# Attention with a top-1 expert branch on one core: the split of the row maxima put ahead of the pair's transfer, and the layernorm's inverse root moved to GpSimd

## The chip, the core and the metric

One core of a Trainium2 chip runs the whole kernel. The metric is device time in microseconds (us) for one execution, inputs and outputs in the chip's memory; lower is better. Engines are named as the profile names them: PE is TensorE's matmuls and PEld its weight loads, DVE is VectorE, ACT is ScalarE, POOL is GpSimd, SP is SyncE, which here only issues transfers.

## The reference

The input x has shape (4, 2048, 512), float32. It is layer-normalised without scale or offset; the attention of 16 heads of width 32 and a top-1 mixture of 8 experts with room for 100 tokens each both read the normalised tokens, and the output is the sum of x and both.

```python
def _layernorm(x, axis=-1, eps=1e-05):
    m = jnp.mean(x, axis=axis, keepdims=True)
    v = jnp.var(x, axis=axis, keepdims=True)
    return (x - m) / jnp.sqrt(v + eps)
...
        scores = jnp.einsum('bhqd,bhkd->bhqk', q, k) / math.sqrt(dh)
        attn = jax.nn.softmax(scores, axis=-1)
        out = jnp.einsum('bhqk,bhkd->bhqd', attn, v)
...
    x = L0_attn_x
    xn = _layernorm(x, axis=-1)
    x = x + _L0_attn_ref(xn, ...) + _L0_ffn_ref(xn, ...)
```

Queries and keys also pass a spectral filter, which the kernel folds into their weights at the start. The softmax subtracts each row's maximum before it exponentiates.

## The kernel before, in words

**Tiling.** The attention is done for one batch and four heads at a time: 4 x 4 = 16 such groups, `k` from 0 to 15. A group has four blocks of 512 queries (`n`), so there are 64 blocks. A block runs over 16 key tiles of 128 keys, two by two: an `even` and an `odd` tile make a window, 8 windows to a block, 512 in all. Scores stand with keys on the partitions and queries along the row.

**One window** (the loop at line 908). For each of its two tiles and each half of the four heads, PE first writes the negated row maxima into the PSUM bank (`shift`, line 614: a matmul with ones against `negms`, a bfloat16 tile), then adds the scores (`scores`, line 603). ACT exponentiates the bank into the tile (line 930). PE multiplies the tile before with the values (`products`, line 630), and DVE adds the result into `num`. For the softmax's sums, the pair of tiles is added: `pair` (line 892) is a transfer issued on POOL that adds the 1 MB `odd` tile onto the `even` one, and `add_to` (line 895) adds the even tile of the window before onto it, mostly on POOL. `odd` tiles have three buffers, `even` tiles five.

**The maxima** are computed ahead. A list `stream` (line 449) has one item for every 128 queries by 512 keys by two heads; the first 40 items run before the window loop (line 788), and after that each half of a tile does one item (`max_matmuls` on PE, `max_reduce` on DVE), so that the maxima of a block are complete some windows before it starts. When a block's 32 items are done, `max_negate` reduces them on DVE, and a window later `max_close` (line 489) turns them on PE and lets ACT copy them twice, as bfloat16 into `row[:, 0]` and as float32 into `rest`. In the window after that, `max_split` (line 501) takes them apart into three bfloat16 parts: two subtractions and two casts on POOL, with three small transfers of 4 KB on SP that spread the three rows into `negms`, the first for ACT's copy, the second and third behind POOL's casts.

**What sets the order.** The engines behind `on` are wrapped by `InOrder` (line 71): each keeps the order in which the program was written, and nothing is rescheduled. So the order in the window loop is the order of POOL's queue: at the head of a window first `pair` (line 910), then `max_split` if a block's maxima are due (line 912), then `add_to` (line 914). What else is to be done is in `agenda`, a list of steps for each window which `plan` (line 841) fills: projections of the next group, loads of weights, the closing of a block (`close_steps`, line 649), the tokens of the next batch. Half of a window's steps follow its even tile, half its odd tile.

**The token stage** (line 221) normalises a batch: `load` (1 MB of x on SP), `measure` (mean and variance on DVE into `mv`), `scale` (line 244: the inverse root of the variance into `rstd`, and `shift`, minus the mean times it), `normalize` on ACT and `turn`, which transposes on PE into `xnT`. For batch 0 this is the start of the kernel, with `scale` for four tiles of tokens at a time and `shift` on DVE (lines 739 to 756). For the other batches it lies in the agenda over the last two groups of the batch before; `scale` then runs once for 16 tiles, with `shift` on POOL. The expert branch gathers at most 800 tokens (7 tiles) and has a `scale` of its own (line 551). ACT's `Sqrt` and `Exp` are in different tables, so that a table load stands before the first Sqrt at the start, and before and after each Sqrt between exponentials. At item 30 of the first loop a one-element `Exp` (line 792) brings in the table of the exponentials early.

Of the kernel before, what the change touches and what calls it, by code (L numbers as in the profile page):

```python
# [12 lines left out]
F32 = mybir.dt.float32  # L13
BF16 = mybir.dt.bfloat16
I32 = mybir.dt.int32
AF = mybir.ActivationFunctionType
ALU = mybir.AluOpType
# [8 lines left out]
P = 128  # L26
NT = S // P
# [7 lines left out]
ST = -(-SLOTS // P)  # L35
NTAB = 4
FAR = 1 << 20
EPS = 1e-5
# [63 lines left out]
def attention_and_top1_experts(ctx: ExitStack, tc: tile.TileContext, a: dict, out: bass.AP):  # L102
    nc = tc.nc
# [4 lines left out]
    const = ctx.enter_context(tc.tile_pool(name="const", bufs=1))  # L108
# [8 lines left out]
    def bank():  # L117

        return array[:, next(turns), :]
# [18 lines left out]
    ones = const.tile([P, P], F32, name="ones")  # L138
    nc.gpsimd.memset(ones, 1.0)
    ones_b = const.tile([P, P], BF16, name="ones_b")  # L140
    nc.gpsimd.memset(ones_b, 1.0)
    eps = const.tile([P, 1], F32, name="eps")
    nc.gpsimd.memset(eps, EPS)

    carry = const.tile([P, E], F32, name="carry")
    nc.gpsimd.memset(carry, 0.0)
# [9 lines left out]
    def chunk(name):  # L156
        tag, bufs = ("y", 1) if name == "y" else ("xs", None)
        return chunks.tile([P, TQ, DM], F32, tag=tag, name=name, bufs=bufs)
# [25 lines left out]
    on = SimpleNamespace(sync=nc.sync)  # L184
# [36 lines left out]
    def token_stage(b):  # L221
        stats = small.tile([P, NT, 6], F32, name="stats")
        mv = small.tile([P, NT, 2], F32, name="mv")
        rstd = small.tile([P, NT], F32, name="rstd")
# [18 lines left out]

        def scale(first=0, last=NT, shift_on=None):
            at = slice(first, last)
            on.scalar.activation(rstd[:, at], mv[:, at, 1], AF.Sqrt, bias=eps[:, 0:1])
            on.vector.reciprocal(rstd[:, at], rstd[:, at])
            if shift_on:
                shift_on.scalar_tensor_tensor(
                    out=shift[:, at], in0=mv[:, at, 0], scalar=-1.0, in1=rstd[:, at], op0=ALU.mult, op1=ALU.mult  # L250
                )
                return
            on.gpsimd.tensor_tensor(shift[:, at], mv[:, at, 0], rstd[:, at], ALU.mult)
            on.gpsimd.tensor_scalar(shift[:, at], shift[:, at], -1.0, None, ALU.mult)
# [205 lines left out]
    def max_matmuls(item, half):  # L460
        k, n, m, t, u = item
        for h in range(2):
            at = DH * (2 * u + h)
            on.tensor.matmul(
                array[:, half[h], :],
                lhsT=qs[k, n][at : at + DH, t * P : (t + 1) * P],
                rhs=ks[k][at : at + DH, m * QB : (m + 1) * QB],
                start=True,
                stop=True,
            )  # L470
# [13 lines left out]
    def max_negate(k, n):  # L484
        negs[k, n] = small.tile([P, HG * TQ], F32, name="neg")
        part = parts.pop((k, n)).rearrange("p h t m -> p (h t) m")
        on.vector.tensor_reduce(negs[k, n], part, AX.X, ALU.max, negate=True)
# [13 lines left out]
    def max_split(k, n):  # L501

        rest, row = closed.pop((k, n))
        for i in (1, 2):
            on.gpsimd.tensor_tensor(rest, rest, row[:, i - 1, :], ALU.subtract)
            on.gpsimd.tensor_copy(row[:, i, :], rest)
        negms[k, n] = qkv.tile([P, QB], BF16, tag="negm", name="negm", bufs=3)
        for i in range(3):
            on.sync.dma_start(out=negms[k, n][i::DH, :], in_=row[:, i, :])


    taken = {}

    def expert_steps():


        def begin():
            w_exp = chunk("w_exp")
            on.sync.dma_start(out=w_exp, in_=a["L0_ffn_w_expert"].rearrange("(r p) n -> p r n", p=P))
            b_exp = work.tile([P, DM], F32, tag="b_exp", name="b_exp", bufs=1)  # L520
            on.sync.dma_start(out=b_exp, in_=a["L0_ffn_b_expert"].partition_broadcast(P))
            entries = small.tile([P, NTAB, ST, 2], F32, name="entries")
            for i, table in enumerate(tables):
                on.sync.dma_start(out=entries[:, i], in_=table.rearrange("(t p) c -> p t c", p=P))
            entry = small.tile([P, ST, 2], F32, name="entry1")
            for i, op in enumerate((ALU.min, ALU.max)):
                on.vector.tensor_reduce(
                    entry[:, :, i], entries[:, :, :, i].rearrange("p n t -> p t n"), AX.X, op
                )
            who = small.tile([P, ST], I32, name="who")  # L530
            on.vector.tensor_copy(who, entry[:, :, 0])
            xg = [chunk("xg"), small.tile([P, ST - TQ, DM], F32, name="xg1")]
            for half in xg:
                on.gpsimd.memset(half, 0.0)
            mv = small.tile([P, ST, 2], F32, name="mv1")
            index = [bass.IndirectOffsetOnAxis(ap=who[:, i : i + 1], axis=0) for i in range(ST)]
            bound = {"bounds_check": B * S - 1, "oob_is_err": False}
            taken.update(mv=mv, w_exp=w_exp, b_exp=b_exp, entry=entry, index=index, bound=bound, xg=xg)

        def row(i):  # L540
            return taken["xg"][i // TQ][:, i % TQ, :]

        def fetch(i):
            on.gpsimd.indirect_dma_start(row(i), None, rows, taken["index"][i], **taken["bound"])

        def measure(i):
            stats = small.tile([P, 6], F32, name="stats1")
            on.vector.bn_stats(stats, row(i))
            on.vector.bn_aggr(taken["mv"][:, i, :], stats)

        def scale():
            rstd = small.tile([P, ST], F32, name="rstd1")
            on.scalar.activation(rstd, taken["mv"][:, :, 1], AF.Sqrt, bias=eps[:, 0:1])
            on.vector.reciprocal(rstd, rstd)
            shift = small.tile([P, ST], F32, name="shift1")
            on.gpsimd.tensor_tensor(shift, taken["mv"][:, :, 0], rstd, ALU.mult)
            on.gpsimd.tensor_scalar(shift, shift, -1.0, None, ALU.mult)
            taken.update(rstd=rstd, shift=shift)

        def expert(i):  # L560

            if i >= 2:
                at = slice(i - 2, i - 1)
                pe = bank()
                for r in range(NR):
                    on.tensor.matmul(
                        pe,
                        lhsT=taken["xt"][:, r * P : (r + 1) * P],
                        rhs=taken["w_exp"][:, r, :],
                        start=(r == 0),  # L570
                        stop=(r == NR - 1),
                    )
                on.vector.tensor_tensor(row(i - 2), pe, taken["b_exp"], ALU.add)
            if 1 <= i <= ST:
                px = bank()
                for r in range(NR):
                    on.tensor.transpose(px[:, r * P : (r + 1) * P], row(i - 1)[:, r * P : (r + 1) * P], ident)
                taken["xt"] = work.tile([P, QB], F32, tag="byx", name="xt", bufs=1)
                on.scalar.copy(taken["xt"], px)
            if i >= 2:  # L580
                on.scalar.activation(row(i - 2), row(i - 2), AF.Copy, scale=taken["entry"][:, at, 1])
            if i < ST:
                at = slice(i, i + 1)
                on.scalar.activation(
                    row(i), row(i), AF.Identity, bias=taken["shift"][:, at], scale=taken["rstd"][:, at]
                )

        return begin, fetch, measure, scale, expert

    def gather_row(i):  # L590
# [197 lines left out]
    for i, item in enumerate(stream[:MAX_AHEAD]):  # L788
        if i == 30:

            early = small.tile([P, 1], F32, name="early")
            on.scalar.activation(early, eps, AF.Exp)
        half = next(turns), next(turns)
        max_matmuls(item, half)
        max_reduce(item, half)
        if i in ahead:
            ahead[i]()
        while full_blocks:
            closing[i + 2] = full_blocks.pop(0)
            max_negate(*closing[i + 2])  # L800
        if i in closing:
            max_close(*closing[i])
            max_split(*closing[i])
# [88 lines left out]
    def pair(first, second):  # L892
        on.gpsimd.dma_start(out=first, in_=second, accum_op=ALU.add)
# [5 lines left out]
    pairs, adds, full, splits = {}, {}, {}, {}  # L899
    left = None  # L900
    window = 0
    maxima = stream[MAX_AHEAD:]
    for k in range(B * NG):
        plan(k)
        for n in range(NQ):
            num = work.tile([P, QB], F32, tag="num", name="num")
            tiles = {}
            for w in range(NW):
                even, odd = w * WIN, w * WIN + 1
                if window in pairs:  # L910
                    pair(*pairs.pop(window))
                if window in splits:
                    max_split(*splits.pop(window))
                if window in adds:
                    add_to(*adds.pop(window))
                here = agenda[window]
# [83 lines left out]
```

## Time and profile before

| | |
|---|---|
| median of 3 runs | 4525.47 us (4524.64 to 4526.17) |
| the profiled execution's own time | 4519.14 us |
| its span, first to last instruction | 4517.2 us |
| mean granted clock of TensorE | 0.987 |
| DMA packets | 707.03 MB, mean 157 GB/s |
| pair transfers on POOL | 510 of 1 MB, 8.1 us from issue to landing (median) |
| `even` added on POOL, 128x1024 | 876 of 2517 ns, 2118.2 us busy |
| exponentials on ACT, 128x512 | 4096 of 601 ns |
| subtract and cast of the split, 16x128 | 128 of 417 ns and 128 of 287 ns (mean) |
| table loads on ACT | 11 of 1283 ns |
| Sqrt of 128x4, 128x16, 128x7 | 8 of 284 to 309 ns |

A line of the profile's groups names the engine, the operation and the tiles (written <- read), the count, and then the busy time, the mean of one in ns, the idle time of the engine just before, and what ended it. Most instructions are issued through the wrapper and so have its line, L82; they are told apart by their tiles. In a timeline a line has the start in us, the duration, engine, operation and tiles, how many alike follow each other (x8), and in brackets the idle time before the first and what ended it. `POOL DMA_DIRECT2D` is the issue of a transfer on POOL, not the transfer; `SPq` is an issue on SP. q0 is the queue of POOL's transfers, q1 that of SP's. [...]

### The profile page before, as it was taken

Reading aid. Unit: us, or ns where it says so; the run is one execution under the profiler, and the core shown is the slowest. Engines: PE = TensorE matmul, PEld = TensorE weight load, DVE = VectorE, ACT = ScalarE, POOL = GpSimd, SP = SyncE. Lnnn points to the kernel's source line nnn. Section 1 sums busy time; section 2 is a strip of 40 time slices with the busy share of each in tenths; the row PEclk is TensorE's granted clock in tenths of the full one; section 3 lists DMA queues with packets and bytes.
Section 4 is the critical chain, followed back from the end, with each engine's and each line's share of the span. In section 5 each row is a group of like instructions: output and inputs, shape, how many; then the busy total and the mean of one; then the engine's idle time right before and its main releaser. Section 6 shows DMA issues by size and latency. Waiting matters only on the chain. (4 is left out here: it accounts for less than half of the span.)

```text
span 4517.2 us, 106256 instructions
## 1 busy us (share of the span) xinstructions
PE 4390.0 (97%) x44398; PEld 1883.0 (42%) x44398; DVE 3134.8 (69%) x3642; ACT 2596.8 (57%) x4988; POOL 2919.2 (65%) x1993
## 2 busy tenths in 40 slices
PE   8999999999999999999999999999999999999998
PEld 4343433434434343444444434343443434434432
DVE  6667667766676777776666766677667765777776
ACT  3455555575555555557555555556655555555555
POOL 0677666765766666775676656667567665776673
PEclk9999999999999999999999999999999999999999
DMA  4677778886777777897677777789767866787778
GB/s 107 157 165 156 152 144 163 196 196 129 144 153 149 145 156 152 167 215 168 131 147 149 159 140 142 156 177 208 160 130 159 167 141 127 149 169 157 149 157 176
DMA packets 191546, 707.03 MB, mean 157 GB/s; under 512 B 47374, under 2 KB 52656, under 8 KB 125784
## 3 DMA queue, kind: packets, MB, share of 16 engines
q0 software_dynamic: 110432, 605.83, 68.9%
q1 hardware_dynamic: 79456, 93.89, 6.7%
q8 instruction: 347, 5.69, 0.5%
q14 instruction: 135, 1.11, 0.1%
q10 hardware_dynamic: 1176, 0.52, 0.0%
HBM read 76.03 MB, written 89.98 MB: 37 GB/s over the span
## 5 line engine op out<-in xcount | busy, mean ns | idle before, releaser
L82 DVE TENSOR_REDUCE part<-array 128x2 f32<-128x1024 f32 (+1 forms) x2313 | 2434.8, 1097 | 1251.7 <-PE array L82 1239.6
L82 PE MATMUL array<-k,q 32*128 32x512 f32 x8192 | 2242.4, 626 | 4.6 <-issue 2.2
L82 POOL TENSOR_TENSOR even<-even 128x1024 f32<-128x1024 f32 x876 | 2118.2, 2517 | 183.0 <-DMA even<-odd 181.8
L82 PE MATMUL array<-q,k 32*128 32x512 f32 x8192 | 2068.7, 598 | 0.8 <-issue 0.8
L82 ACT ACTIVATE even<-array 128x512 f32<-128x512 f32 x2048 | 1066.3, 601 | 540.9 <-PE array L82 536.7
L82 ACT ACTIVATE odd<-array 128x512 f32<-128x512 f32 x2048 | 1060.1, 602 | 429.0 <-issue 221.4
L82 POOL DMA_DIRECT2D even<-odd x510 | 442.0, 867 | 1227.6 <-ACT odd L82 1032.7
L82 PEld LDWEIGHTS array<-k,q 32*128 32x128 f32 x8192 | 811.3, 185 | 165.6 <-DVE num L82 68.4
L82 PE MATMUL array<-negm,ones_b 3*128 3x512 bf16 x4096 | 799.1, 384 | 78.7 <-DMA negm<-row 70.5
L82 PEld LDWEIGHTS array<-q,k 32*128 32x128 f32 x8192 | 755.3, 187 | 16.5 <-issue 6.8
L82 DVE TENSOR_TENSOR num<-num,array 128x512 f32<-128x512 f32 x960 | 651.2, 678 | 50.5 <-PE array L82 31.2
L82 PEld LDWEIGHTS <-ones_b 3*128 3x128 bf16 x4096 | 203.4, 92 | 968.7 <-issue 805.5
L82 PE MATMUL array<-even,v 128*32 128x512 f32 x4096 | 549.6, 607 | 14.4 <-ACT odd L82 14.4
L82 PE MATMUL array<-odd,v 128*32 128x512 f32 x4096 | 555.3, 613 | 4.7 <-ACT even L82 4.5
L82 PE MATMUL array<-xnT,wg 128*32 128x512 f32 x4096 | 465.5, 595 | 1.3 <-ACT xnT L82 0.7
L82 PE MATMUL array<-wo,ot 128*32 128x512 f32 x2048 | 259.3, 596 | 1.7 <-POOL ot L82 1.7
L82 PEld LDWEIGHTS array<-xnT,wg 128*32 128x32 f32 x4096 | 132.7, 111 | 307.2 <-issue 271.1
L82 PEld LDWEIGHTS array<-odd,v 128*32 128x32 f32 x4096 | 81.9, 109 | 405.6 <-ACT even L82 397.2
L82 PEld LDWEIGHTS array<-even,v 128*32 128x32 f32 x4096 | 81.1, 108 | 406.4 <-ACT odd L82 393.5
L82 PEld LDWEIGHTS array<-wg,xnT 128*32 128x32 f32 x8192 | 226.2, 110 | 41.4 <-issue 23.8
L82 PE MATMUL array<-wg,xnT 128*32 128x128 f32 x8192 | 235.7, 273 | 1.9 <-issue 1.9
L82 ACT COPY y<-array 128x512 f32<-128x512 f32 x252 | 147.7, 586 | 138.3 <-PE array L82 137.7
(127 smaller groups left out, 1354.5 us busy)
## 6 DMA issues: line engine op xcount, KB each, us to landing
even<-odd POOLq DMA_DIRECT2D x510, 1024.0 KB, 8.1
out_dram<-y POOLq DMA_DIRECT2D x63, 1024.0 KB, 12.1
xs<-in_L_attn_x_dram SPq DMA_DIRECT2D x30, 1024.0 KB
out_dram<-xs SPq DMA_DIRECT2D x16, 1024.0 KB
factor<-inverse SPq DMA_DIRECT2D x248, 64.0 KB
wg<-wd SPq DMA_DIRECT2D x15, 768.0 KB
wo<-in_L_attn_w_out_dram SPq DMA_DIRECT2D x16, 256.0 KB
negm<-row SPq DMA_DIRECT2D x192, 4.0 KB
```

Of the source, the lines that this page charges most:

```text
L82: done = act(*args, **kwargs)
```

## The change

At the head of a window the split now comes before the pair. And the inverse root is computed on POOL as (variance + eps) to the power -0.5, with a constant tile of exponents; ACT's Sqrt and DVE's reciprocal are gone, with the table loads around them. The early `Exp` reads another constant, as `eps` is no longer a tile.

```diff
-    eps = const.tile([P, 1], F32, name="eps")
-    nc.gpsimd.memset(eps, EPS)
+    power = const.tile([P, NT], F32, name="power")
+    nc.gpsimd.memset(power, -0.5)
...
         def scale(first=0, last=NT, shift_on=None):
             at = slice(first, last)
-            on.scalar.activation(rstd[:, at], mv[:, at, 1], AF.Sqrt, bias=eps[:, 0:1])
-            on.vector.reciprocal(rstd[:, at], rstd[:, at])
+            on.gpsimd.tensor_scalar(rstd[:, at], mv[:, at, 1], EPS, None, ALU.add)
+            on.gpsimd.tensor_tensor(rstd[:, at], rstd[:, at], power[:, at], ALU.pow)
...
             rstd = small.tile([P, ST], F32, name="rstd1")
-            on.scalar.activation(rstd, taken["mv"][:, :, 1], AF.Sqrt, bias=eps[:, 0:1])
-            on.vector.reciprocal(rstd, rstd)
+            on.gpsimd.tensor_scalar(rstd, taken["mv"][:, :, 1], EPS, None, ALU.add)
+            on.gpsimd.tensor_tensor(rstd, rstd, power[:, 0:ST], ALU.pow)
...
-            on.scalar.activation(early, eps, AF.Exp)
+            on.scalar.activation(early, ones[:, 0:1], AF.Exp)
...
                 even, odd = w * WIN, w * WIN + 1
+                if window in splits:
+                    max_split(*splits.pop(window))
                 if window in pairs:
                     pair(*pairs.pop(window))
-                if window in splits:
-                    max_split(*splits.pop(window))
                 if window in adds:
```

On the engines, the built programs differ in this: POOL's queue has the four instructions of the split ahead of the pair's issue in 63 places (block 0's split lies before the window loop and is unchanged) and 16 more instructions for the eight inverse roots. ACT has eight Sqrt and nine table loads less, DVE eight reciprocals less. The orders on PE and SP are the same.

## The prediction

> **What bounds the kernel now.** I read the page first, then the waits, then the timeline around the longest wait, then the DMA view and the windows view there. The chain that ended last holds only the final few microseconds and says nothing here. The page:
>
> ```profile
> span 4517.2 us, 106256 instructions
> PE 4390.0 (97%) x44398; PEld 1883.0 (42%) x44398; DVE 3134.8 (69%) x3642; ACT 2596.8 (57%) x4988; POOL 2919.2 (65%) x1993
> ```
>
> PE (TensorE's matmuls) is busy for 97%; what can be won is its idle time, and time in which it is busy at a lower clock. The waits:
>
> ```profile
> PE array L82 <- DMA negm<-row: 70.5, 22, 7.0
> PE array L82 <- ACT odd L82: 14.4, 11, 2.2
> POOL even L82 <- ACT odd L82: 1032.7, 307, 12.1
> ```
>
> (waiting instruction <- releaser: us in total, times, longest.) Of some 114 us of PE idleness between matmuls, 70.5 us in 22 waits are for one small transfer: the negated row maxima, which the first `shift` matmul of a block of 512 queries needs. There are 64 such blocks (I count from 0), so about every third stalls. The timeline of block 61 on POOL, then PE:
>
> ```profile
> 4315.71 4.68 POOL L82 TENSOR_TENSOR even<-even 128x1024 f32<-128x1024 f32 x2 [3.59 <-DMA even<-odd]
> 4320.33 0.84 POOL L82 DMA_DIRECT2D even<-odd  x1
> 4320.91 0.42 POOL L82 TENSOR_TENSOR rest<-rest,row 16x128 f32<-16x128 f32 x1
> 4321.40 0.28 POOL L82 CAST row<-rest 16x128 bf16<-16x128 f32 x1
> 4321.76 0.42 POOL L82 TENSOR_TENSOR rest<-rest,row 16x128 f32<-16x128 f32 x1
> 4322.24 0.28 POOL L82 CAST row<-rest 16x128 bf16<-16x128 f32 x1
> ```
>
> ```profile
> 4327.71 0.61 PE L82 MATMUL array<-negm,ones_b 3*128 3x512 bf16 x2 [4.97 <-DMA negm<-row]
> ```
>
> The pair's 1 MB transfer is issued at 4320.33, the four instructions of the split follow and end at 4322.52, SyncE issues the last row at 4322.55, and PE gets it only at 4327.71, 5.2 us later. The DMA view of 4321.6 to 4326.7 and of the microsecond after it (queue: packets, MB, share) says why:
>
> ```profile
> q0 software_dynamic: 128, 1.05, 101.2%
> ```
>
> ```profile
> q1 hardware_dynamic: 40, 0.01, 4.4%
> ```
>
> In the first stretch only the pair's 128 packets move; every packet of the two rows (q1) stands behind them. In block 0, where no pair is under way, the last row is issued at 94.45 and PE starts at 96.70: 2.25 us. So the pair costs a row 3 us, and the split before it on POOL stands behind the pair as well.
>
> The third view is the windows view after the stall of block 20 (3.43 us):
>
> ```profile
> 1490.90:1497.70 6.80, 6.21 (x32) 2.64 (x36) 2.46 (x3) 2.17 (x4) 4.87 (x3) 0.50 0.80 161
> 1497.70:1504.50 6.80, 6.80 (x64) 2.41 (x60) 3.10 (x4) 3.75 (x7) 1.81 (x3) 1.00 0.00 0
> ```
>
> The second column after the stretch is PE with its number of matmuls; 0.50 and 1.00 are the granted clock. After the stall 6.8 us pass at half clock and 32 matmuls run where 64 run next: 3.4 us more are lost. The records show 121 us at half clock in all (mean 0.987); about 88 us of that follow the 22 stalls, a loss of 44 us. [...] I count the half-clock stretches as recorded.
>
> **The split ahead of the pair.** Nothing is added or removed: two subtracts (0.42) and two casts (0.28), 1.60 us with their gaps, change places with one issue (0.6 us until POOL goes on). SyncE's order is the same; its row transfers are only released earlier, with what stands behind them. The split needs ACT's copies of `row` and `rest`, done 3.3 us before the odd exponentials for which the pair waits. But POOL isn't free for all of that: it still adds. New start of the split = the later of ACT's copy and the end of POOL's work before the pair. Block 8: copy at 645.66, POOL's adds end 647.74, so 647.74 to 649.34 instead of 649.58 to 651.18: 1.84 us earlier. Block 16: POOL is busy until 1215.87, so 0.59. For the 22 stalled blocks it is 0.5 to 1.9 us: little.
>
> The larger part is the queue. The last row would be issued 0.03 us after the split, and its first packet comes 1.17 us after its issue (block 0). The pair would be issued as the split ends, and its first packet comes 1.43 us later (median of 148 pairs issued while the engines were quiet). So the row is ahead by about 0.2 us, and it lands 2.25 us after its issue instead of 5.2. [...] I take the row of block 61: first to arrive goes first.
>
> Need against arrival: the stalled blocks want the maxima 9.03 us after ACT's copy in most cases. New arrivals are (split's end) 3.7 to 5.9 + 2.3 = 6.0 to 8.2. So:
> - 16 blocks of the ordinary kind: 44.5 us of stalls go, but for 0.3 (block 24, behind the 768 KB of `wg`).
> - Blocks 60, 61, 63 (4.1 + 5.0 + 7.0 = 16.1 us): POOL is free only 5.2 to 6.7 us after the copy; arrivals are 0.3, 1.5 and 4.5 late. 9.8 us go.
> - Blocks 12, 28, 44 (3.5 + 3.6 + 2.7 = 9.9 us): there the next 1 MB of x stands ahead of the rows on the same queue, and even the first row, issued early, takes 7.5 to 9.8 us to its first packet. These I leave: 0.
>
> Sum 54 us. With these stalls go some 60 us of half-clock stretches (3.4 or 6.8 each): 30 us.
>
> What it costs: the pair starts up to 1.6 us later (block 16: 1217.5 for 1215.9). Next on POOL are adds whose start doesn't move, since split and pair precede them either way. The pair's landing (8.1 us on the page) is wanted one window, about 8.2 us, later, so POOL may wait up to 1.6 us more there. Cover: POOL waits 1032.7 us in all for exponentials, 2 us a pair. Taken as 0; if the cover were gone, see the third rival.
>
> **The inverse root.** Removed: nine of eleven table loads of 1283 ns, eight Sqrt of 0.3 us on ACT, eight reciprocals of 0.2 us on DVE. Added on POOL: eight adds (nearest row: a scalar operation of 128x16 at 0.27 to 0.31 us) and eight powers. No row shows a power. Lower bound: a two-operand POOL instruction of this shape, 0.22 us; below that there is nothing, as an instruction is added. [...] I take 0.5 us.
>
> Mid-kernel the loads stand between two tiles of exponentials:
>
> ```profile
> 923.29 1.28 ACT L82 ACT_TABLE_LOAD   x1
> 924.59 0.31 ACT L82 ACTIVATE rstd<-mv,eps 128x16 f32<-128x16 f32 x1
> 924.92 1.28 ACT L82 ACT_TABLE_LOAD   x1
> ```
>
> PE then waits 1.61 to 1.64 us, four times. Three of these lie just before the waits of blocks 12, 28 and 44, which I leave; there the maxima merely get waited for longer. The fourth counts: 1.6 us. On POOL add and power come before `shift`, which ends at 931.46, while the first normalisation runs at 943.27: 11.8 us of cover. Behind them stand `ot` (wanted by PE 4.6 us after its end) and a pair: hidden up to some 4 us. At the start the chain runs mv 21.92, table load, Sqrt, reciprocal, shift 24.96, normalisation 24.99; ACT would be free at 22.95. With add and power on idle POOL the shift is ready at about 23: 2 us, and 0.7 us on each of three further groups, partly hidden: 3 us. [...]
>
> **Sum.** 54 + 30 + 1.6 + 3 = 89 us against the profiled execution's 4519.1 (span 4517.2 and 1.9 around it). The median of the runs, 4525.5, lies 6.3 us above; the same difference gives 4436.5, I say 4437.
>
> **Rivals.**
> - The x queue clears too (chance 0.10): blocks 12, 28, 44 lose their 9.9 us, 4.9 us of table waits and 8.5 us of half clock: 4413. For it: less traffic in front. Against: the first row's own 7.5 us.
> - The rows still stand behind the pair (0.22): a lead of 0.2 us is small. Then only the earlier split counts, the smaller of lead and stall in 19 blocks: 19 us; shorter stalls save about 10 us of clock; with 4.6 for the root: 4491.
> - The change doesn't do what it says (0.06): the maxima were not late but something just behind them is; the waits are renamed: about 4520.
> - Slower (0.10): the pair's delay takes the place of the wait. Place: POOL's adds, and through the buffers that they free the exponentials and PE. Price: up to 1.6 us in 63 blocks, 101 us, with half clock after some. It decides once POOL's wait for exponentials falls below 1.6 us a window, as it does where POOL is already waiting for a pair (block 61 above: 3.59). All 63 together, against 89 gained and with 30 of clock given back: about 4568.
> The main case holds 0.52.
>
> About 0.2% is what a measurement of this kernel can tell from no change. Faster 0.86, within it 0.05, slower 0.09. The range leaves out the last two rivals: 4408 to 4493.
>
> **What would show it.** Right: the waits of PE for `negm` fall from 70.5 to about 16 us, in blocks 12, 28, 44, 61 and 63; a mean clock of 0.993 or 0.994; last row to matmul 2.3 us; two table loads; powers of about 0.5 us. Wrong: 5 us from the last row to the matmul still (second rival), more of POOL's waiting for `even<-odd` than 191.5 us and PE waiting for exponentials (slower), or powers of many microseconds.

## The result, and the profile after

The changed kernel takes 4455.08 us (median of 4 runs, 4451.27 to 4463.09) against 4525.06 (4 runs, 4524.62 to 4526.17): a ratio of 0.9847, 95% interval 0.983 to 0.9864, some 70 us less. The execution that was profiled took 4463.09 us, the longest of the four, so its span falls by only 55.9 us. Its page:

```profile
span 4461.3 us, 106253 instructions
PE 4369.7 (98%) x44398; PEld 1869.5 (42%) x44398; DVE 3130.6 (70%) x3634; ACT 2581.3 (58%) x4971; POOL 2958.8 (66%) x2009
```

PE is busy 20.3 us less, with the same number of matmuls, and idle between them for 79 us where it was 114. The mean granted clock (TensorE's, which the profile gives as a share of full speed) rises from 0.987 to 0.993. The waits, the same view as before:

```profile
PE array L82 <- DMA negm<-row: 4.6, 3, 3.0
PE array L82 <- POOL ot L82: 37.4, 15, 6.8
PE array L82 <- ACT odd L82: 8.3, 8, 2.2
POOL even L82 <- ACT odd L82: 887.8, 262, 11.9
POOL even L82 <- DMA even<-odd: 241.8, 167, 6.9
```

The wait for the maxima has gone from 70.5 us in 22 stalls to 4.6 in 3. PE's wait for `ot` (the product `num` x `factor`, which closes a block and is made on POOL) was this before:

```profile
PE array L82 <- POOL ot L82: 1.7, 1, 1.7
```

It is now 37.4: about half of the idle time that was won came back under another name. POOL waits less for exponentials (1032.7 before) and more for its pairs (191.5).

Block 61 on POOL, then PE's next stall there:

```profile
4267.53 4.67 POOL L82 TENSOR_TENSOR even<-even 128x1024 f32<-128x1024 f32 x2 [3.57 <-DMA even<-odd]
4272.16 0.42 POOL L82 TENSOR_TENSOR rest<-rest,row 16x128 f32<-16x128 f32 x1
4272.64 0.28 POOL L82 CAST row<-rest 16x128 bf16<-16x128 f32 x1
4273.00 0.42 POOL L82 TENSOR_TENSOR rest<-rest,row 16x128 f32<-16x128 f32 x1
4273.48 0.28 POOL L82 CAST row<-rest 16x128 bf16<-16x128 f32 x1
4273.98 0.88 POOL L82 DMA_DIRECT2D even<-odd  x1 [0.21 <-ACT odd L82]
...
4279.20 1.57 POOL L82 TENSOR_TENSOR ot<-num,factor 128x512 f32<-128x512 f32 x1
```

```profile
4280.82 1.07 PE L82 MATMUL array<-wo,ot 128*32 128x512 f32 x8 [2.10 <-POOL ot L82]
```

The split now ends before the pair's issue. The last row's first packet comes 1.16 us after the row's own issue; before it was 4.30 in this block. Over all 64 blocks the median of that time falls from 4.40 to 1.16 us: before, 62 blocks were above 4 us, now none is, and 52 are at 1.3 or less. In this block the pair is issued 0.21 us after the split ends, and its first packet comes 0.48 us after the row's first one; the row's last packet has come by then (1.27 us after the row's issue). What is left in this block is a wait of 0.88 us for the maxima, which ends at 4275.51, and the stall of 2.10 us for `ot`, behind POOL's adds.

The three longest new stalls are those of blocks 12, 28 and 44. This is block 12, where the inverse root of the next batch runs on POOL as well:

```profile
915.22 4.68 POOL L82 TENSOR_TENSOR even<-even 128x1024 f32<-128x1024 f32 x2 [3.50 <-DMA even<-odd]
920.00 0.27 POOL L82 TENSOR_SCALAR rstd<-mv 128x16 f32<-128x16 f32 x1
920.35 2.94 POOL L82 TENSOR_TENSOR rstd<-rstd,power 128x16 f32<-128x16 f32 x1
...
923.94 1.26 POOL L82 TENSOR_TENSOR ot<-num,factor 128x512 f32<-128x512 f32 x1
```

```profile
925.25 2.79 PE L82 MATMUL array<-wo,ot 128*32 128x512 f32 x12 [6.21 <-POOL ot L82]
```

POOL waits 3.50 us for its pair, adds for 4.68, spends 3.9 on the inverse root and `shift`, and only then divides. PE has been idle for 6.21 us by then; in blocks 28 and 44 it is 6.75 and 5.96 us. The windows view of the 6.8 us from there, with the same columns as before:

```profile
925.20:932.00 6.80, 6.75 (x40) 2.38 (x44) 1.16 (x2) 2.21 (x5) 5.57 (x4) 0.61 1.00 269
```

The granted clock falls to a mean of 0.61 after this stall, as it fell after those for the maxima. The powers, by shape (count, us busy, mean ns):

```profile
L82 POOL TENSOR_TENSOR rstd<-rstd,power 128x16 f32<-128x16 f32 x3 | 8.8, 2943 | 0.2
L82 POOL TENSOR_TENSOR rstd<-rstd,power 128x4 f32<-128x4 f32 x4 | 4.2, 1041 | 0.3
L82 POOL TENSOR_TENSOR rstd<-rstd,power 128x7 f32<-128x7 f32 x1 | 1.5, 1517 | 0.1
```

Two table loads are left of eleven.

### The profile page after: what moved, and what is told of

It reads as the page before. It is cut to its first block, busy times and chain, and to the rows that moved or that the text cites. A ratio compares the mean times of both kernels' runs of the same rounds, so it can differ in the third digit from the quotient of the medians.

```text
span 4461.3 us, 106253 instructions
## 1 busy us (share of the span) xinstructions
PE 4369.7 (98%) x44398; PEld 1869.5 (42%) x44398; DVE 3130.6 (70%) x3634; ACT 2581.3 (58%) x4971; POOL 2958.8 (66%) x2009
## 5 line engine op out<-in xcount | busy, mean ns | idle before, releaser
L82 PE MATMUL array<-q,k 32*128 32x512 f32 x8192 | 2047.3, 593 | 1.3 <-issue 1.3
L82 POOL DMA_DIRECT2D even<-odd x510 | 460.1, 902 | 1101.7 <-ACT odd L82 887.8
L82 PE MATMUL array<-negm,ones_b 3*128 3x512 bf16 x4096 | 792.4, 382 | 15.6 <-issue 5.2
L82 PEld LDWEIGHTS array<-q,k 32*128 32x128 f32 x8192 | 746.0, 185 | 13.2 <-issue 4.3
L82 PE MATMUL array<-wo,ot 128*32 128x512 f32 x2048 | 264.4, 607 | 37.5 <-POOL ot L82 37.4
```

What stands on the lines that cost most here:

```text
L82: done = act(*args, **kwargs)
```

## The experiments

My theory (A): the row's place in the DMA queue is the whole gain; what is missing went to `ot`, which stands on POOL behind adds that wait for the pair. Rival (B): the earlier split on POOL's own queue is what helped, not the transfers. Rival (C): the inverse root has its own part in the gain, through the table loads. The recorded expectations letter some of these otherwise: in those of e1 and e2, theory B is rival C here; in that of e5, theory D is rival B; theory C in e3, e4 and e7 says that `ot` only shows a wait that has another cause. "Before" on the three chips used took 4520.99, 4527.12 and 4524.08 us (medians of 27, 9 and 9 runs); each ratio is against it on the same chip.

**First chip. e1_split_only**: before, with the split ahead of the pair, and nothing else of the change.

```diff
                 even, odd = w * WIN, w * WIN + 1
+                if window in splits:
+                    max_split(*splits.pop(window))
                 if window in pairs:
                     pair(*pairs.pop(window))
-                if window in splits:
-                    max_split(*splits.pop(window))
```

> The kernel before with the split put ahead of the pair, and nothing else: Sqrt and its table loads stay. Theory A (the queue): the time comes from the split alone, PE's waits for negm fall from 70.5 us to below 10, and the last row lands about 2.3 us after its issue; PE instead waits for ot on POOL, some 30 us (less than the 37.5 of the changed kernel, as no power of 2.9 us stands ahead of ot), while the four table-load stalls of 1.6 us come back: 4450 to 4465. Theory B (the gain comes from ACT's relief by the inverse root): no more than 15 us faster than before, 4510 to 4525.

Measured: 4448.03 us, ratio 0.9836 (0.9823 to 0.9849). PE's waits:

```profile
PE array L82 <- POOL ot L82: 19.2, 15, 2.7
PE array L82 <- ACT odd L82: 14.5, 11, 2.2
PE array L82 <- DMA negm<-row: 9.0, 3, 4.9
```

The time lies just below the range of A and far from that of the expectation's theory B. The split alone brings the whole gain; C falls. It also brings 15 stalls for `ot` (19.2 us, where 30 were expected), so these are not the root's. In block 12 its `ot` stall is 0.81 us and in block 28 1.58. In block 44 it has none, but there PE has stood 4.92 us for the maxima already, which covers `ot`. A second execution of this kernel, e9 below, has no such stall and waits 1.18, 1.63 and 0.61 us for `ot` in these blocks: 3.4 us, where the changed kernel has 18.9. The 15.5 us between them are about what add and power (3.3 us of POOL each time) and the missing table stall (1.6 us, by which PE comes earlier) make together.

**e2_root_only**: before, with the root on POOL, and the split left behind the pair.

```diff
-            on.scalar.activation(rstd[:, at], mv[:, at, 1], AF.Sqrt, bias=eps[:, 0:1])
-            on.vector.reciprocal(rstd[:, at], rstd[:, at])
+            on.gpsimd.tensor_scalar(rstd[:, at], mv[:, at, 1], EPS, None, ALU.add)
+            on.gpsimd.tensor_tensor(rstd[:, at], rstd[:, at], power[:, at], ALU.pow)
```

> The kernel before with the inverse root as a power on POOL, and nothing else: the split stays behind the pair. Theory A: the negm waits stay at about 70 us and cover the power; 2 to 8 us faster than before (the fourth table stall of 1.6 us, the start, 1 to 5 us of the others): 4517 to 4524. Theory B: most of the 70 us: 4455 to 4465. A third possibility, that the power costs: its 2.9 us on POOL in blocks 12, 28 and 44 push the pair and ot back, 0 to 10 us slower than before.

Measured: 4521.37 us, ratio 0.9998 (0.9987 to 1.0009). PE's wait for the maxima, and its stall of block 12:

```profile
PE array L82 <- DMA negm<-row: 74.8, 22, 7.1
```

```profile
929.24 0.61 PE L82 MATMUL array<-negm,ones_b 3*128 3x512 bf16 x2 [5.65 <-DMA negm<-row]
```

The table stall of 1.6 us is gone, and the stall for the maxima just behind it is 5.65 us where it was 3.54: the same deadline, waited for longer. By itself the root is worth nothing that can be measured.

**e3_ot_on_vector**: the changed kernel with `ot` divided on DVE instead of POOL, so that nothing on POOL stands ahead of it.

```diff
-            on.gpsimd.tensor_tensor(held["ot"], num, held["factor"], ALU.mult)
+            on.vector.tensor_tensor(held["ot"], num, held["factor"], ALU.mult)
```

> The changed kernel with the product ot = num x factor on DVE instead of POOL, all else in place. Theory A (what was not gained is the new wait of PE for ot behind POOL's adds, 37.5 us in 16 places with 27 us of half clock after them): that wait goes to below 5 us and the time to 4400 to 4420, as in DVE's queue ot stands behind reductions of 1.2 us and not behind adds of 5 us; DVE's 63 products of 0.7 us, 43 us at 70% busy, are hidden. Theory C (the missing gain is something else, for instance the pair's delay or the DMA queues, and ot only shows it): the wait is renamed and the time stays within 10 us of 4455.

Measured: 4520.71 us, ratio 1.0003 (0.999 to 1.0015). The expectation is missed by a hundred microseconds: all that the change won is lost. DVE and POOL in one stretch, and the group:

```profile
2171.29 5.83 DVE L82 TENSOR_TENSOR ot<-num,factor 128x512 f32<-128x512 f32 x1
```

```profile
2171.60 4.96 POOL L82 TENSOR_TENSOR even<-even 128x1024 f32<-128x1024 f32 x2
```

```profile
L82 DVE TENSOR_TENSOR ot<-num,factor 128x512 f32<-128x512 f32 x63 | 138.1, 2192 | 0.6 <-DMA factor<-inverse 0.6
```

Where POOL adds nothing, this product takes DVE 0.684 us (15 of the 19 that lie clear of POOL's adds are at 683 to 686 ns). Where it lies wholly beside POOL's adds it takes up to 5.83: it began before the two adds and ended half a microsecond after them. DVE's addition of the same size into `num` has one input in PSUM and keeps its 678 ns (median of 960 in e3, 627 to 689). Behind the slow products stand DVE's reductions of the maxima: PE's waits for them (`part`) grow to 36.9 us, those for `ot` are still 22.1, and 101 us run at half clock. So e3 says nothing for or against A; it moved the product to a worse queue.

**e4_ot_before_adds**: the changed kernel, `ot` still on POOL, but issued at the head of its window, ahead of the adds.

```diff
+                if window in divides:
+                    divides.pop(window)()
                 if window in adds:
                     add_to(*adds.pop(window))
...
-                    at(window + after, *step)
+                    if after == 7 and len(step) == 1 and step[0].__name__ == "divide":
+                        divides[window + after] = step[0]
+                        at(window + after, lambda: None)
+                    else:
+                        at(window + after, *step)
```

> The changed kernel with ot put ahead of the window's adds in POOL's queue (split, pair, ot, adds); no engine gets other work. Theory A: as with ot on DVE, PE's wait for ot falls below 5 us, 4400 to 4420; POOL's adds start 1.3 us later in 62 windows, which its waits for exponentials (887.8 us) cover. Theory C: within 10 us of 4455. If ot then waits for the factor's transfer, POOL's waits show it as a wait for DMA factor.

Measured: 4432.87 us, ratio 0.9802 (0.9789 to 0.9815). The direction is right, about half of the size came. In block 12 `ot` starts without a wait right behind the pair's issue and ends 5.8 us before PE uses it; PE's wait for it is back at 1.7 us in all. But four stalls for the maxima stand for 13.0 us: in blocks 28, 40 and 44 the last row's last packet comes 7.5, 6.4 and 9.5 us after its issue (1.27 where nothing is in the way), and PE stands for 4.21, 2.50 and 5.88. And PE waits 16.7 us for `part` on DVE. The longest of these, DVE and PE:

```profile
4229.55 0.25 DVE L82 RECIPROCAL few<-few 128x16 f32<-128x16 f32 x1 [7.33 <-DMA few<-sums]
```

```profile
4230.93 0.58 PE L82 MATMUL array<-negm,ones_b 3*128 3x512 bf16 x1 [6.21 <-DVE part L82]
```

DVE stands 7.33 us for a small transfer (`few`, issued at 4219.73), the reductions stand behind the reciprocal in DVE's order, and PE behind these. The pattern is the old one: a small transfer that comes late, and an engine in program order behind it.

**Second chip. e5_small_pair**: before, with the order unchanged and no root; the pairs of those windows that have a split are cut to 256 of their 2048 columns, so the softmax's sums lack the rest of these pairs.

```diff
+                    first, second = pairs.pop(window)
+                    if window in splits:
+                        first, second = first[:, 0, 0, 0:256], second[:, 0, 0, 0:256]
+                    pair(first, second)
```

> The kernel before, with its order (pair, then split) and its Sqrt, but in the 63 windows with a split the pair's transfer moves an eighth: 256 of 2048 columns, 128 KB for 1 MB. Left out: the rest of those pairs, so the softmax's sums lack them. Theory A (a row waits in the DMA queue behind the pair's 1 MB): the split stands where it stood, about 3.3 to 6.7 us after ACT's copy, but its last row lands 2.3 to 3 us after its issue instead of 5.2, and PE's waits for negm fall from 70.5 us to below 25; 4440 to 4475. Theory D (what counts is the place in POOL's order, that is the 0.5 to 2.3 us by which the split itself starts earlier): the waits stay above 50 us and the time above 4500.

Measured: 4435.81 us, ratio 0.9803 (0.9786 to 0.9821). PE's wait for the maxima:

```profile
PE array L82 <- DMA negm<-row: 5.9, 2, 4.5
```

POOL splits behind the pair as before, but only an eighth of the bytes stand ahead of its rows, and the last row's first packet comes after 1.16 us (median; 4.40 before). That decides between A and B: it was the queue. (The time itself is a little below the range of A.) PE waits 13.9 us for `ot` here too, so these waits come whenever the stall ahead of them goes, not from the pair's later start alone. Part of them does hang on the pair: in blocks 4, 16, 32 and 48 they are 0.6 us each, where e1 has 1.2.

**e6_split_ot**: before, with the split ahead of the pair and `ot` ahead of the adds, the root left on ACT and DVE (the diffs of e1 and e4 together).

> The split ahead of the pair and ot ahead of the window's adds, without the inverse root: Sqrt, its reciprocals and its table loads as in the kernel before. If the root is worth its table loads once ot no longer stands behind the power (theory R): slower than with the root (0.9802 of before), by the four table stalls of 1.6 us and the start: 0.981 to 0.984 of before. If the root brings nothing in any order (theory N): 0.979 to 0.981.

Measured: 4430.61 us, ratio 0.9785 (0.9768 to 0.9802), the fastest of its chip, and a little below both ranges. Theory R, that the root is worth its table loads here, falls.

**e7_four_more_powers** and **e8_changed_again**: the changed kernel with four more powers of 128x16, whose results nobody reads, at the end of each mid-kernel `scale`; and the changed kernel itself on the same chip.

```diff
+            spare = small.tile([P, NT], F32, name="spare")
+            for _ in range(4):
+                on.gpsimd.tensor_tensor(spare, rstd, power, ALU.pow)
```

> The changed kernel with four more powers of 128x16 into a spare tile after shift in the three mid-kernel scales, 11.8 us of POOL ahead of ot in blocks 12, 28 and 44; nothing else moves. Theory A (POOL's time ahead of ot goes one for one into PE's wait): the three waits for ot grow from 6.2, 6.8 and 6.0 us to about 18 each, 35 us in all, plus half clock of up to 10: 4490 to 4505. Theory C (ot is only where the wait shows, the cause being a transfer or an exponential): less than 15 us slower than the changed kernel.

> The changed kernel itself, beside the others on one chip, to compare it with the split alone (0.9836 of before) and with the split and ot without the root. If the root costs in the changed kernel what its powers add to the waits for ot (37.5 against 19.2 us) less its table stalls (6.5 us): 0.985 to 0.987 of before. If it neither gains nor costs: 0.983 to 0.985.

Measured: 4497.63 us, ratio 0.9941 (0.9922 to 0.9959), and 4462.51, 0.9861 (0.9843 to 0.9879), both where theory A and a root that costs put them. In e7 PE waits for `ot`:

```profile
PE array L82 <- POOL ot L82: 62.0, 13, 17.9
```

Twelve powers of 2.91 us are 34.9 us more on POOL; the time rose by 35.1, and PE's wait for `ot` by 34.1 (27.9 in e8). In blocks 12, 28 and 44 nothing covers `ot` any more: in these runs a microsecond on POOL ahead of it was a microsecond of the kernel. Block 28 shows the cover at work: in e8 PE stands there 5.53 us for the maxima and then not at all for `ot`, in e7 5.78 and then 10.95, while the profile after had 0.67 and then 6.75.

**Third chip, all four combinations: e9_split_2x2** (as e1), **e10_changed_2x2** (the changed kernel), **e11_ot_first_2x2** (as e4), **e12_split_ot_2x2** (as e6).

> The split alone once more, beside the changed kernel, ot-first and split with ot-first without the root on one chip, so that the root's worth can be read in both orders. If effects add (from the two earlier chips: ot first -23, root +8 us): 8 us faster than the changed kernel. If the root is neutral: within 3 us of it.

> The changed kernel on the same chip: root cost +8 us against the split alone if the powers ahead of ot are what it costs; within 3 us if the root is neutral.

> The changed kernel with ot ahead of the adds. If the root's cost is only its standing ahead of ot, it is gone here: at or below split with ot-first without the root (by up to 6 us, its table stalls). If the root costs POOL in any place: 3 to 10 us above it.

> Split and ot-first without the root: 0.9785 of before on another chip; here the same within its interval, 20 to 26 us below the split alone.

| | root on ACT and DVE | root on POOL |
|---|---|---|
| split first | e9: 4450.17, 0.9839 (0.9826 to 0.9853) | e10: 4456.41, 0.9855 (0.984 to 0.987) |
| split first, `ot` first | e12: 4433.6, 0.9798 (0.9784 to 0.9811) | e11: 4441.83, 0.9814 (0.9801 to 0.9828) |

`ot` first is worth 16.6 us without the root (20 to 26 were expected) and 14.6 with it. The root costs 6.2 us (8 were expected if it costs), and 8.2 with `ot` first (3 to 10): the intervals of each pair touch, the sign is the same in both. That it costs something with `ot` first as well means that its place ahead of `ot` isn't all of it; the profile of e11 has more waiting for the maxima (15.6 us) than that of e12 (6.1), but such waits differ by several microseconds between profiles of one kernel (e10's 10.4 and e8's 7.4 against 4.6). I leave that cause open. The line of e10:

```profile
PE array L82 <- DMA negm<-row: 10.4, 3, 6.4
```

## Why the prediction was right, and where it was off

- **Mechanism of the split: right.** The row ahead of the pair gets its first packet 1.16 us after its issue, as block 0 had it. The rival that rows still stand behind the pair fell, by the profile after and by e5. Behind the pair the row's first packet came 4.40 us after its issue at the median, 3.2 more than the 1.17 us of block 0; ahead of it, in block 61, the whole row had passed, 1.27 us after its issue, before the pair's first packet. The lead was not the 0.2 us that I reckoned but about half a microsecond (0.47 to 0.51 in 22 blocks, more in 24), since the pair is issued 0.21 us after the split's end and not with it.
- **Stalls for the maxima: 54 us expected to go, 66 went.** In the profile after, the blocks 12, 28 and 44, which I left at zero, lost nearly all of theirs (0.67 us left, in block 28), and block 60 all of it. Their first row, issued early, does wait 7.2 to 7.8 us in the profile after, but the last row, on which all hangs, gets its first packet 3.3 to 3.7 us after its issue where it was 6.1 to 7.5. I had carried the first row's wait over to the last. But this profile was lucky in part. In two other executions of the same kernel, e8 and e10, the last row of block 28 had its first packet after 4.2 to 4.3 us too, yet its last packet only after 9.39 and 9.77 us (4.21 in the profile after), and PE stood 5.53 and 6.43 us for it. Such late last packets, 6.9 to 10.6 us, also come in one or more of blocks 12, 28 and 44 in e1, e4, e6, e11 and e12; what decides when they come is not shown. So 60 to 66 us went.
- **Half clock: 30 us expected, 29 measured** (121.5 us of half-clock stretches became 62.9, and half of the difference counts). Of these some 3 us were no loss, as PE stood idle for 15.6 us of the half clock before and for 9.6 after. What is left follows the stalls for `ot` in part. By the same records a gap of 2.27 us cost clock before and one of 3.03 us did not; see the last section.
- **Table loads: 1.6 us expected, 6 measured.** All four stalls of 1.6 us went (PE's wait for `odd` 14.4 to 8.3), since the stalls that would have swallowed three of them went too. e2 shows the other case: with those stalls in place it is nothing.
- **The head: 3 us expected, 0.5 measured.** Block 0's first matmul came at 96.22 us where it had come at 96.70; as e1 (root as before) has 95.12 and e10 (root changed) 94.19, this is within what executions differ by. `shift` was ready at 24.63 where it was 24.96, with statistics that came 1.0 us later. The powers of 1.04 us take back much of what the table load gave.
- **The power: sized at 0.5 us, measured 1.04, 1.52 and 2.94**: above the lower bound of 0.22 us, and six times my value for the form that matters. No run shows the 0.5 us, which was a guess; the profile after shows 1041, 1517 and 2943 ns for 4, 7 and 16 columns. The four of 128x4 took 1037 to 1049 ns, and the first was the longest by 8 ns.
- **The step that failed** is "`ot` (wanted by PE 4.6 us after its end) ... hidden up to some 4 us". That cover was read from a trace in which the stall that I was removing supplied it. In block 12 of before:

```profile
931.47 0.61 PE L82 MATMUL array<-negm,ones_b 3*128 3x512 bf16 x2 [3.54 <-DMA negm<-row]
...
937.32 1.77 PE L82 MATMUL array<-wo,ot 128*32 128x512 f32 x10
```

```profile
931.40:937.30 5.90, 5.83 (x28) 2.45 (x32) 2.52 (x3) 2.17 (x4) 5.90 (x5) 0.50 0.79 200
```

`ot` ended there at 932.70, 4.6 us ahead of its matmul. But PE had come 3.54 us late because of the stall, and the 5.85 us from the stall's end to that matmul ran at a clock of 0.50, which is 2.9 us more. Without both PE wants `ot` 6.4 us earlier, that is, 1.8 us before it is there, with no power and no later pair at all. The split alone, e1 and e9, did stall for `ot` in this block, for 0.81 and 1.18 us; with the power it was 6.21. The rest of the trace says the same: of the 15 stalls for `ot`, one (1.7 us in block 63) was there before; the other 14 lie in 14 blocks, and each of these had stalled for the maxima before. The pair's later start, which I took as 0 under "what it costs", was judged by POOL's waits for exponentials, and PE's need of `ot` behind POOL's adds was not looked at; e1 against e5 puts its part at some 0.6 us in blocks 4, 16, 32 and 48. The price of the new waits is 37.4 - 1.7 = 35.7 us in the profile after (27.9 and 27.2 in place of 37.4 in e8 and e10, where the maxima cover block 28).

Put together on the profiled executions: 66 + 29 + 6 + 0.5 - 36 = 65.5 us, against 55.9 in the span. PE's idle time fits (114 to 79). The remaining 9 us are in PE's busy time, which fell by 20.3 where 29 of half clock went; the 3 us at which PE was idle are part of them, and the other 6 I haven't placed. Two errors thus stood against each other: 12 + 4 us more were gained than I reckoned, and 36 us of new waits were not in the sum at all. That the predicted 4437 is only 18 us below the 4455 measured is in part luck. The slower rival had the right queue, POOL's adds behind the pair, but the wrong victim: PE waits for `ot`, in 14 blocks, not for exponentials in all 63.

The version that the runs point to is the split ahead of the pair and `ot` ahead of the adds, with the root left where it was: 0.9785 (0.9768 to 0.9802) and 0.9798 (0.9784 to 0.9811) of before on two chips. What it still waits for, the late `few` and the late rows of some blocks, wasn't taken further.

## What to carry to other kernels

Before you call a later wait covered, take the stall that you remove, and its half clock (in block 12 3.54 and 2.9 us), out of that cover: what is late next may be what the stall had been hiding. Issue the small transfers on which an engine waits ahead of a large one that shares the DMA engines, even by a fraction of a microsecond (0.48 us in block 61, for 1.16 us to the row's first packet instead of 4.30); and then look at each in-order queue for the next instruction that stands behind the large one's landing. An operation whose cost no row shows, put on the queue of a busy engine, should be given a wide range and counted at its upper end where something on the path stands behind it (0.5 us counted here, 2.94 measured).

## What was not expected of the hardware

- DVE's product of two tiles in SBUF, 128x512, took 0.684 us alone and up to 5.83 beside POOL's adds in e3; the adds themselves hardly slowed (4.96 us for two, against 4.68 before).
- POOL's powers in the profile after fit 0.41 us and 0.16 us per column (1041, 1517 and 2943 ns for 4, 7 and 16 columns of 128 partitions); its product of 128x16 took 0.215 us there.
- Half a microsecond of lead at the DMA queues (0.48 us in block 61) went with 3 us less waiting: 1.16 us to the row's first packet in the profile after against 4.40 before, at the median.
- In the profiles before and after, the half clock goes with slices of time and not with the length of a gap alone. All half-clock stretches begin and end on one grid of 3.413 us, to within 1 ns, but for the end of the record. Before, from 41 us on, the clock fell from full to half 22 times; in 21 of the slices just ahead PE was busy for 0.00 to 0.46 of the time (0.78 in the other, at 98.3 us), while no slice that kept the full clock behind it was below 0.51. A gap of 2.27 us at 1221.54 lies within one slice; one of 3.03 at 175.11 is cut at 176.8 into 1.66 and 1.37 us. The border isn't the same in every trace: after, eleven of the twelve falls lie behind slices of 0.00 to 0.49 and no slice that kept the clock is below 0.50, while in e8 it stayed full after one with 0.41.
